# A four-layer graph network on one core: TensorE's large operations planned in two parts, with a new order table

## The chip, the cores and the metric

The kernel runs on one core of a Trainium2 chip. The metric is the device time of one execution in microseconds (us), as the median of several runs. The engines are named as in the profile: PE is TensorE's matrix multiplication, PEld its weight loads, DVE VectorE, ACT ScalarE, POOL GpSimd and SP SyncE, which here only issues DMAs.

## What is computed

There are 16 graphs of 1024 nodes with 256 features each (float32), and one adjacency matrix of 1024 x 1024 for all. Four layers follow each other. Each normalises x, applies a ReLU and adds the result of a graph layer:

```python
h = jnp.maximum(_layernorm(x, axis=-1), 0.0)
x = x + _L0_gnn_ref(h, adj, L0_gnn_W, L0_gnn_a)    # and so on: L1, L2, L3
```

Layers 0 and 1 are graph attention with one head. The score of a pair is the sum of a term of each node, and the weights are masked by adj and normalised over the neighbours:

```python
h = jnp.matmul(inp, W)
e = jax.nn.leaky_relu(e_src[:, :, None] + e_dst[:, None, :], negative_slope=ALPHA)
e = jnp.where(adj[None, :, :] == 0, NEG_INF, e)
h_prime = jnp.matmul(jax.nn.softmax(e, axis=-1), h)
```

Layer 0 ends in a ReLU, layer 1 in an ELU. Layer 3 is the same with four heads of 64 features and an ELU. Layer 2 is a transformer block: queries, keys and values from one 256 x 768 matrix, eight heads of 32 features, scores q k / sqrt(32) masked by adj, softmax, sum with the values, a layer norm, a feed-forward part (256 to 256, ReLU, 256 to 256) and another layer norm.

## The kernel before

**Stages.** A stage is one layer of one graph, so there are 64. `order` (L1844 on) interleaves them: in the middle of the run, layer 2 of graph b, layer 1 of graph b+1, layer 3 of graph b and layer 0 of graph b+2 follow each other, and the preparation of a later stage overlaps the main part of an earlier one.

**Way in** (`way_in`, L1100). Each tile of 128 nodes gets its moments (DVE L1047, L1048, or ACT L1071), the inverse root on POOL (L1051 and L1052, or L1074 and L1075) and the normalisation (ACT L1135 or L1151, DVE L1144). Four tiles, half a graph, make one call of `transpose_rows` (L1083): eight PE transposes (L1090) into one pair of PSUM banks, which ACT empties into `hT` (L1093). Then come the projections, all through `project` (L1095, its matmul is L1097): `gat_values` (L1194) two tiles at a time for layers 0, 1 and 3; `two_values` and `queries_keys` for layer 2. ACT or DVE empties each product's bank pair.

**Main part.** Layers 0 and 1 (`gat_item`): DVE makes the weights p of a tile of neighbours (L1362), PE multiplies them with the values (av, L1379), and ACT and DVE finish each tile (L1396 to L1422) and hand it to the next layer's way in. Layer 3 (`pair_item`): weights on DVE (L1443), values and sums as 32-column matmuls that run four at a time (L1477, L1501). Layer 2 (`dot_item`): PE makes the scores of four heads as four concurrent 32-row matmuls into two pairs of banks (sc, L1597), ACT exponentiates them (L1611), DVE masks them (L1619), and PE multiplies with the values (acc, L1628). Every second time POOL issues a DMA that adds one block of weights to the next (L1645), and a matmul forms the sums of what has landed (L1658). After the last neighbour `dot_out` normalises, and `feed_forward` (L1739) and `finish` do the rest: transposes, the up product with ACT's ReLU (L1774), the down product with DVE's addition (L1797), the second layer norm (L1812, L1819).

**Buffers.** PSUM's eight banks are two single accumulators ("acc") and three pairs ("u"). Transposes, projections and scores all take pairs from these three, and one score operation takes two.

**What sets the order.** Nothing is issued in the order in which the code above is written. Each piece of work is an `op` with an engine, a cost in us, a rank, the operations that it comes after, and the buffers that it takes and ends. After all are collected, `play` (L941) runs `forward` (L839), a planner that lays the operations out in time engine by engine with these costs, with `DELAY` (L769) from the end of an operation to its users on other engines, and with `SWITCH` (L772) added on PE when the form of the matmuls changes (full, 32 rows, 32 columns):

```python
DELAY = (0.2, 0.12, 0.14, 0.06, 2.0, 1.4)   # PE, DVE, ACT, POOL, SP, QUEUE
SWITCH = {None: 0.2, 132: 0.21, 32: 0.125}
```

Of the operations that could begin within `SLACK` (0.5 us) of the earliest, the one with the lowest rank goes first. The instructions are then issued in the planned order. The ranks come from the text `RANKS` (L47), three characters for each operation; it is used if its length is three times the number of operations, and otherwise `play` makes ranks by planning forward and backward eight times. QUEUE is not an engine but the planner's picture of POOL's DMA queue: the adding DMA is planned as 0.9 us on POOL with a delay of 0.6, then 5.2 us of QUEUE and its delay.

Of the kernel before, what the change touches and what calls it, by code (L numbers as in the profile page):

```python
# [28 lines left out]
U8 = mybir.dt.uint8  # L29
# [3 lines left out]
AX = mybir.AxisListType  # L33
PSUM = bass.MemoryType.PSUM

P = 128
# [11 lines left out]
    "$7K#`;$57#};#U[#8d#-f##%###$'v#;a#.U##$#$5#$&$6j#Pq#$(#cE##E#$W#$<#xV##=#%#$Jw#$;##,#$H#$o#+$#Jm#$w#+d##+#%?$1;"  # L48
    "#H)#&R#')#'C#'O#'.#':#'R#'b##f#+###3##r$=O##I##j#*}##H##v#*b#Tz#cL#`U##0##6##C#$I#$G#$T#Gf#$7##5#$F#iA#$_##-#%)"
    "##y#ok##F##|##G##h#$'#`@#*-#$-#*i#`R#S$#WI#$}#%U##4#%x#$[#$Z##z#$E#$i#$2#%p#we#$O#%t#*j#*`#$A##&#$C#)>$&R$<_#vY"  # L50
    "$<6#JZ#%V#)u#)2#$K#(K#(-#wg#%h#&4#&%#&]##x#$Q##u##.#%l#%z#$@##P#$|#''#$a#-m#$]#]<#'?#%:#$D$BL#$j#]:#%7#&Y$H;#&8"
    "#%D$19#$:#AB#%u#&?#}=#&S#%9#%_#',#&A#'-#&q#v_#$P##Y#&B#%i#&w#'g#&`#'7#%n#'I#_p#L=#b##$h#$p##L#$u#$q#$y#%%#$L##W"
    "#%-#%W#%<#%`#'a#'6#&(#%3#%d#&t#cA#%J#&H#A:##R#%[#%k##9#'U#%s##`#,L#'&##S#%g#$4#'`#%B#%v$#8##c#%f#&z#c:#$e$Iu#Xf"
    "$*R#&9#%}#Xg#&:#_/$-O#uE#%G#*g#EY#T8#ui#$c$CA$H8#$n#3%#Tp#%F#2b#%@#${$Ew#&C##b#%M#$f#$0#%H#$z#$%#%/#$l#%4#$M#%N"
    "#%8#%e##(#&I#%+#t<#j?#%,$.f#&M#%.#2?#]0##n#'E#$v#%$#$t#$m#%m#%^#'j#(m#'H#(d#$x#&*#&[#&o#%q##J#']#-@#%P#%1#'Q#vX"
    "#EX#:B#$.#%I##7#$d#%a##_##8#$3#'W#'{#&'#/r#%=#az$KE#$b#'4#L`#$$#b$#0:#_0$*r#R9#$##&m#+q#*$#09#&u$*q$Kt#&1#'>#05"
    "$7h#R8#%0##a#0F#[F#'T#&i#$J#G>#&e#_g#ov#(,#GS#(}$:)#&K#%r#&^#%A#&n#&&#%&#$B$8R#&v$Ks#&j$LG#Fy#'%#JJ#&/#)P#&$$(M"
    "#&p$08#uH#tF#o7#)O#&F#%o#%b#&+#*(##X$9B#&>#%O$9##'|$9Y#DY#$>#'P#'_#'l#(5#)@#'}#?+#%6#(6#Y.#[N#[M#<R#0j#(##%2#q_"
    "#qN$9n#*M##K#&c#&b#'=#$R#1Q##Z##2#o4#$*#($#$?#(/#%R$9p#oM#&V#I8#-2#DZ#Kr#1d#,B#&G#'9#Jq#*q#$8$9v$:_#y7#6?#'f#K="
    "#(s#r:#(r#'*$Bb#_s$%L#([#JM#(<#AL#(I#w_#r5#&E#&P#(%#,_#(*#VI$+d#'c#'q#KL#.-#(f#-V$4l$Je#'r#((#;3#H+#<&#)#$?&#AO"  # L60
    "#ck#(8#&O#vO#83$5F$:^$7.#(.#(C#&g#(J#&=#(R#)K#(V#(l#(U#)0#)%#)|#)D#)S#+2#;7#%w#&a#$)#'1#&_#%*#$`#(7#(X#%y#(y#i*"
    "#&h#u,#re#(_#(W$0=$23$0<#&U$FK#&T#(L#(2#K##(D$/n#)r#0n#(A#(v#(N$0;#)q#(0#)p#0m$8Y#)3#)-#Gq#4f#)x#)E$$A#=Q#G]#'L"
    "#i+#H8#'d$3a#Jy#()#)/#)8#'t#)b#(a$8u#vv##B#)1#)9#D,#)g#,q##A#vo##@#)6#)Y#)7$Ho#)+#QW#uq#),#(@#)d#'F#$N#)*$=##)C"
    "#+k#*:#*s#,g#-r#+0#71#0t#0(#(|#q<#D4#pz#D:#*>#)R$6w#(e#QZ#D(#,.#)G#`-#*T#*9#*a#.j#,1#*B#*H#*l#Dk#LC#*'#-j#*W#'["
    "#u4#*Q#*4#{s#-h#D3#9J#*_#*J#p|#B##La#.8#*v$5.#7I#+4#*[#eE#.D$IK#*u#*U#*S#)h#.>#(P#.<#*X$;}#+B#=B#+R#*h#nE$+q#(O"
    "##]#*f#*]$5?$Ij$M.#+m#+>$5%#u3#+Q#+<$L]#>x#Ig#+l#*V#+=#/'#[p$B@#<;#+^$-|#Y_#+Y#*%$B?#zG#XR#K{#+L#+&#+c$O%#+j#<_"
    "#+i$4}$<>#+u#*y#)_#y($Ai#}A#+g#+]$C,$6m#Wb#L%#,,#M=#aC#{a#+5#rn#,>#C/#+`#+[$Ek#?>#*8#,f$0H##D#)4#)T#*K#+|#jE#+%"
    "#&X#,n$G;#,'#(G#..#e2#+b$7r#?k#Qu#)L#g9#*m#on#nl#.Z#+-#=R#Jt#.'#.]#-x#.H$E4#H@#-U#-a#/_#.G#.P#0.#-]#l;#*x#/V#/L"
    "$(9#.O$OJ$Dr#.I#/f##<#0B#.N#^T#/9#.*#-W#.r#.9#1)#0<#/U#.S$A:#D1#fV#;2#/3#.;#+,#+*$<H#y)#Va$9G#+f#,/$Ah#*<#LD$7-"
    "#,*#VV#T&#,9#-+$?)$Bc#M<#C'#{>#)W#rY#Cn$:i#Cm#,C$-{#T%#,o#,7#/,$7D#4e#+C#,^#,6#/.#+a$:h#)}#,v#aB#['#,V#+M#&W#,N"  # L70
    "#0g#?R#-Q#,d#.,#,;#+)#?Q#-O#0-#(F$Oa#+O#+.#(h#,}#*P#,u$Dz#-$#.0#,Z#l4#-&#,D#+9$7;#-?#,j#(g#-%#]s#,0$/$#+w#m:#,h"
    "#]e#,8#-=$?3#RV#0D#-N#nI$Mt$7v##*$G=#-y#,a#.V#Ht#/4#,M#(`#p9$(y#.J#l<#+1#,W#:a#/b#,e#om#*7#-q#*R#+H$Do#*w#1+#+G"
    "#/z#,l#-u#,z#,|#.R#.$#-(#*/$>o#.a#oP#.:#--#/%#+K#-B#/>#._#-X#.^#o,#.b#.v#Qz#BC#mJ#QP#0h#`=#-G$J{$Kv#(M#&s$5D#.A"
    "#&r#0$#)m#1P#,y$J0#1Z#0+#&-#-w#be#,{#/}#*O#/k#-A#&)#,U#/g#,(#+z#/5#0)#h0#,`#-p#,r#'2#,X#.C#g0#/t#0k#u$#0/#/{#-^"
    "#+_#.{#/6#/K#/Y#/X#1&#*e#.B$,_#]3#_(#oN#(b#0l#VS#)`#)^#*Z#*&#,?$0z#+/#+h#,k#*t#*,#*G#**#*L#(3#8+$8;#*)#+($59$J|"
    "#WB$.g$J_#yG#+e#)n#+:#-;#)o#+3#-e#,O#LX$0E#2J#+D#*A#I3#*z#dg#.=#s,#s-#.w$/X#+E#,J#*C#+7#/+$'I#Tk#A-#)l#+o$6d$#`"
    "#,x#|=#)B#-S#-_#-I#-|#-}#-v#)?#/l#+}##?#0U#S:#^S#0X#2M$(x#-8#.t#.h#9|#-R#mG#ff#.d$CJ#(H#/H#:.#t##/0#/($B;$)K#/#"
    "#[?$=C#[a#-K#/[#.K#.u$7m#,Q$5H#,G#mt#/v#,F#3D$5G#jF$KK$>T#.p#2D#od##>#S;#2E$CI#.q#q^#Kz#.7#0>#//#.E#EF#Sr#0*#hd"
    "#tv#f?#P0#-*#0E#0C#/8#,&#/^#mu$=<#-t#0?#2Y#l&#/J$<;#mA#{f#/o#Ci#-M#8`#1J#3,#29#`D#0L#if#ie#pF#0G#;p#{H#8k#/)#]?"
    "#_<#[z#+;#+Z#+T#+{#30#1*#1i#,R#+N#+U#Do#1;#./#ol#q}#/y#H&#31#qH#-o#)Z#.4#Gk#}x#4K#/T#Yz#0`#0K#15#.[#2o#1j#0H#.&"  # L80
    "$J3#/x#0]#,##+J#/P#/Q$'V#0r#0Z#0z#1?#1$#1F#1R#0[#1/#0f#/$#11#1>#03#5.#1E#1:#2m#1[$N-#1o#0o#@-#(Y#5<#);#b4#1(#aA"
    "#1z#6]#7Y#/1#-c#1Y#^6$JQ#1e#/7#12#1C#Se#2*$;s#@1#H^$*{#0x#-b#0p#9y#1k#?b#/]#1y#(Z#1f$BO$-i#e-#tJ#2&#/&#cO#0S#5;"
    "#1g$1/#2=$Hh#1h#bj#0b$-h$*T$*(#2B$*6$+|#0|$JU#2)#1=$*4#{*#2T$K7#2X#2(#1^#@.#M%#2O#/e#/m#5'#p{#2^#0%#/d#4E#7e$K6"
    "#53#2G$+T$>W#21#1n#/Z#S)#-k#A+#0^#1B#-1#T.#nV#6W#2[#>%$@p#2Z#2'$Iw#58#1`#[-#1s#2C#,t#]b$Iv#,:#4O#46#M'#26#/?#nW"
    "#(k#pq#2$#2:#2Q#oX#^v$$m#.1#3/#Hk#>$$>V#0M#>B#1m#3;#.F#2A#3C#3>#2_#3M#4D#3T#/G#3Q#42#3U$-]#3N#8n#3v#9f#3P#8j#5q"
    "#?I#44#)i#6t##[#2@#`<#4]#(?$1m#5`#4J#*N#4T#33#OG#*Y#7.#:*#,K#50#L1$C4#t'#U+#*E#R*#7)#1D#zf#zI$-u#1I#/A#8.#5X$Cp"
    "#3B#wq#/E#kJ#37#3i#2|$26#4;#7U#35#7^#:>#59$;,#5x#4x#7=#7L#3L#1q#B9#[w#qy$5Z#2h#2N#oL#WY#OF#[v#43$Bg#4s#3##1x#B'"
    "#o6#D7#,5#2d#2f#mK$'$#K,$#o#3.#3t$?6#1|#07#Ju$OZ#?P#3K#^<#2e#bA#32#mM$'G$EU#3[#4r#2z#25#b_#3A$-?#3R#HV#23#1T#3G"
    "$=J#2W#2##+@#3s#L9#4>#3+$M,#3W#2n#3e#2y#3?$*f#3Z$+R#3]#e5#47#$,#5a#3'#-i#34#+?#1l#3^#17#9S#3f#3<#3u#3w$Mg##l#TB"
    "#2x$1Q#3x#4j#41#4&#2w#J6#4-$7G#4I#40#3g#3@#4Z#3m#70#F|$4s#GO#4<#4,$;Q#B>#7/#6O#4|#BQ#4m#<C#uo$Ld#5_$C8#4?#1<#4N"  # L90
    "#24#3d#4P$.*#5C#6s#3=#4l#5Q$8E#5>#80#3O#-F#69#4k#3}#-E#5O#Be$I|#'D$5/#^V#3S#s`#2l#5h#94#1G#76$?T#5W$Ec#7N#1p#5L"
    "#5y#Bm#By#9W#9k#$1#Br#1,#6a#Bl#5V$Eg#6v##o#7?#6w#f@#Av##e#uz#/i#3|#0J#0O$O$#0T#1t#5s#0P#7##2F#V3#0R#Mm$IW#2{#61"
    "#[4#2]#[0$?H$?A$?R#Bs#F{#6(#6P#6'#zP#Mz#6&#4Q#4=#4C#4y$03#7@#(x#4U#oZ#3($A-#5]#1S#l##4B#tj$+P#T2#5%#51$;Y#60#4F"
    "#X%#s@#5)#5B#36#4:$60#Y=#5o#49#5b#1W$1h#nw#5{#9##78#X9#aw#4%#6j#5z#6n#R,$FF#Qw#5H#5S#7R#2R#fi#6|$6$#r0#5R#5j#Bf"
    "$7+#4##7m#77$IX#5n#6-#6z#7(#7A#W=#6b#}t#6Y#75#hw#W2#hv#yy#7$##^#6Q$Bi#Nj#Vr#o5$*x#Dd$3z#5/#5,#4{#5i#0Y#F7#62#5$"
    "#3*#.T#7z#8O#6d#3c#-s#.W#6i#6u#5##5^#.s#.6#6Z#XQ#6m#6x#r)#7B#O:#7u#2S#79#8U#7i#:?#{N#9O#9h#%K#7g#7V#@9#nv#7|#%]"
    "#8G#7[#6^#8;#85#7k#8-#8S#8D#8B#7v#68#9,#M;$9,#TE#8b#?a#8a#;##8H#9&$>)#<q#8J#_q#Lm$'3#HE#,$#7C#2p$4.#7'#k8#nm#7D"
    "##'#Y0#7G#5v#Em#8R$JF#8&#5g#3V#6o#6{#7%#8N#6D#7a#7t#7P#7K#4^#6G#7T#6;$)%#Y@$El#4w#7-#k`#7d#7x#:8$JE#4*#4v#7J$Kh"
    "#9$#l=#5U#8X$1j#7;#7+#7{#4t#3I#4i#:;#SW#G(#45#4h#@]#@[#Ks#:x#9H#;x#9'#x-#x]#;w#:v$<7#7_#Z&#87#d1$@?#g+#d6#6`#8'"
    "#:P#nX#'e#mW$F<#<6#8s#9Z#<p$>-#-4#86$Eh#<)#6N#98#cl#-g#cq#Ln#Ft#;r#9B#0I#9l#8F#9=#9:#:r#:)#9i#9%#2.#2-$N}#5k#74"  # L100
    "#'m#'z#_M#8E#:o#9?#9M$ER#K7$/m#5[#@W$0,#9D#9[#cp#8e$Ej#/R#F.$,u#9g#9A#&k#:l$,t#<##@_#G&#/D$({#'<#;}#xH#9Y#?p#';"
    "#9R#:I#9d#2r#:s#6K#Ab#8K#&2#:H#8u#;o#I>#x'#9Q#:t#93$#a$#n#8P$/p#;V#mX$+G$B0#95#7p#;U$=h$HX#9E#Fe#;s#:e#9z#9<$IZ"
    "#Cj$3S#84#:4#:9#xo#:(#yc#9{#@^#[A#:y#9K#&3#IB#8w#x.#:`##;#8v#I@#7M#um#:k#cB#Z,#;5#9}$16$,Z#QY#=$#;M#6e#Qb#ns$K-"
    "$,Y#:d#8$$Ki#dk#;=#9>#:=#J:#89#?'#9t#6)#:<#jC#9;#em#;@$DX#<A#;C#9u#:c#4[#;N#el#;1#6I#<8#4n$DP#:}#;k#AX#uT#;P#5J"
# [515 lines left out]
def fast_path(tc, bad, x, adj, l0_w, l0_a, l1_w, l1_a, w_qkv, ln1_g, ln1_b, ln2_g, ln2_b, w1, b1, w2, b2, l3_w, l3_a, out):  # L620
# [13 lines left out]
    with ctx:  # L634
# [128 lines left out]

        ops = []
        PE, DVE, ACT, POOL, SP, QUEUE = range(6)

        DELAY = (0.2, 0.12, 0.14, 0.06, 2.0, 1.4)  # L769
        ITSELF = 0.04  # L770

        SWITCH = {None: 0.2, 132: 0.21, 32: 0.125}  # L772


        BEFORE_END = 0.1
# [1268 lines left out]
```

## Time and profile before

| | us |
|---|---|
| three runs | 4212.40, 4209.66, 4214.54 |
| median | 4212.4 |
| the profiled execution, whole | 4213.85 |
| its span, first to last instruction | 4212.1 |
| PE busy | 4093.9 |
| DVE, ACT, POOL busy | 3170.0, 2322.9, 1169.6 |
| PE's waits for the adding DMA (L1658) | 27.8, in 35 waits |
| mean granted clock of PE | 0.994 |

In a line of the groups, the part between "x" and "|" is the number of instructions, then come busy time and the mean of one in ns, then the engine's idle time just before them with what ended it. In a line of the timeline, the first number is the start in us, the second the time from the first start to the last end of the instructions merged in the line, and the bracket holds the idle time before. A float32 matmul is recorded as two instructions. Matmuls overlap in the record, so that the time from one start to the next says more than the length of one. In a line of the stretches, the last three numbers are the granted clock as a share of the full one, the DMA engines' busy share and GB/s; before them stand the length and the busy times of PE, PEld, DVE, ACT and POOL with their counts.

### The profile page before, as it was taken

The numbers are of one execution on the slowest core, as the hardware profiler recorded it, in microseconds if no ns is written. First come the engines' busy times: TensorE is split into PE (matmuls) and PEld (weight loads), VectorE is DVE, ScalarE is ACT, GpSimd is POOL, SyncE is SP. The second block draws the span as 40 slices with busy tenths as digits, with TensorE's granted clock in tenths as the row PEclk, the third lists the DMA queues.
The fourth block names the chain that finished last, engine by engine and source line by source line (L and its number), as shares of the span: only waits on it lengthen the run. The fifth ranks groups of instructions, "written<-read, shape, count | busy, mean of one in ns | idle before, by whom it ended". The sixth has DMA issues, their size and how long they took to land.

```text
span 4212.1 us, 67534 instructions
## 1 busy us (share of the span) xinstructions
PE 4093.9 (97%) x25993; PEld 2160.5 (51%) x25993; DVE 3170.0 (75%) x5964; ACT 2322.9 (55%) x4235; POOL 1169.6 (28%) x2025
## 2 busy tenths in 40 slices
PE   8999999999999999999999999999999999999997
PEld 7735255553555536455364654546545465564433
DVE  7577867778677786777867778776787877859697
ACT  5564645636456364564646646465463745666452
POOL 2322231412314123141331423223132241423131
PEclk9999999999999999999999999999999999999999
DMA  3171814518145181451815518164271733636361
GB/s 124 34 158 35 176 45 96 111 49 170 39 99 107 51 170 36 112 108 37 170 38 116 113 35 162 41 135 91 53 151 33 159 67 79 121 82 132 72 135 47
DMA packets 106826, 398.96 MB, mean 95 GB/s; under 512 B 11528, under 2 KB 47744, under 8 KB 73728
## 3 DMA queue, kind: packets, MB, share of 16 engines
q0 software_dynamic: 46080, 302.01, 36.5%
q1 hardware_dynamic: 60000, 92.03, 6.7%
q8 instruction: 206, 3.38, 0.3%
q14 instruction: 124, 1.02, 0.1%
q10 hardware_dynamic: 416, 0.52, 0.0%
HBM read 107.87 MB, written 18.21 MB: 30 GB/s over the span
## 4 chain that ended last, share of the span: by engine, by line
PE 74%; DMA 7%; DVE 6%; issue 6%; ACT 4%; POOL 2%; SPq 0%; POOLq 0%; ACTq 0%; DVEq 0%
PE pm L1097 19%; PE av L1379 18%; PE acc L1477 10%; PE sc L1597 8%; PE acc L1628 6%; DMA pe<-pe 5%; PE sums L1501 5%; PE sums L1658 3%; PE tp L1090 3%; DVE pe L1619 2%; DMA y<-offsets 2%; ACT pe L1611 1%; DVE y L1797 1%; ACT pm L1071 1%; PE tpv L1540 1%
## 5 line engine op out<-in xcount | busy, mean ns | idle before, releaser
L1619 DVE TENSOR_TENSOR pe<-pe,mask 128x1024 f32<-128x1024 f32 x1024 | 1200.6, 1219 | 208.7 <-ACT pe L1611 205.1
L1611 ACT ACTIVATE pe<-sc 128x1024 f32<-128x1024 f32 x1024 | 998.0, 1022 | 321.0 <-PE sc L1597 228.0
L1379 PE MATMUL av<-v,p 128*128 128x257 f32 x4096 | 956.7, 384 | 21.7 <-ACT o L1402 10.7
L1379 PEld LDWEIGHTS av<-v,p 128*128 128x128 f32 x4096 | 764.9, 191 | 210.9 <-issue 60.8
L1443 DVE SCALAR_TENSOR_TENSOR p<-r,e,mask 128x1024 f32<-128x1024 f32 x512 | 623.0, 1274 | 114.6 <-DMA r<-kept 98.0
L1597 PE MATMUL sc<-qT,kT 32*128 32x512 f32 x4096 | 620.9, 642 | 2.7 <-ACT pe L1611 1.5
L1628 PE MATMUL acc<-pe,v 128*32 128x512 f32 x4096 | 538.3, 604 | 1.3 <-DVE pe L1619 0.6
L1645 POOL DMA_DIRECT2D pe<-pe x256 | 224.7, 878 | 992.5 <-PE acc L1628 628.7
L1074 POOL TENSOR_SCALAR rstd<-stats 128x1 f32<-128x1 f32 x512 | 159.0, 311 | 1153.4 <-ACT xn L1071 739.8
L1477 PE MATMUL acc<-p,v 128*32 128x512 f32 x4096 | 463.0, 593 | 0.0
L1597 PEld LDWEIGHTS sc<-qT,kT 32*128 32x128 f32 x4096 | 189.8, 183 | 379.4 <-issue 174.7
L1097 PE MATMUL pm<-l_wx,hT 128*128 128x259 f32 (+1 forms) x1536 | 369.5, 389 | 8.1 <-ACT hT L1093 5.2
L1362 DVE SCALAR_TENSOR_TENSOR p<-r,e,mask 128x512 f32<-128x512 f32 x512 | 349.1, 743 | 24.8 <-DMA r<-kept 19.1
L1075 POOL TENSOR_TENSOR rstd<-rstd,minus_half 128x1 f32<-128x1 f32 x512 | 331.6, 648 | 42.7
L1097 PEld LDWEIGHTS pm<-l_wx,hT 128*128 128x128 f32 x1536 | 287.4, 191 | 79.1 <-ACT hT L1093 20.7
L1658 PE MATMUL sums<-pe,pick 128*32 128x512 f32 x2048 | 269.5, 603 | 28.6 <-DMA pe<-pe 27.8
L1477 PEld LDWEIGHTS acc<-p,v 128*32 128x32 f32 x4096 | 131.1, 110 | 296.1 <-issue 282.1
L1628 PEld LDWEIGHTS acc<-pe,v 128*32 128x32 f32 x4096 | 94.2, 108 | 339.8 <-issue 206.4
L1051 POOL TENSOR_SCALAR rstd<-stats 128x1 f32<-128x1 f32 x256 | 131.9, 515 | 454.5 <-DVE stats L1048 450.8
L1501 PE MATMUL sums<-p,e 128*32 128x512 f32 x2048 | 242.3, 593 | 0.0
L1097 PE MATMUL pm<-hT,qkv_sb 128*128 128x512 f32 x512 | 228.6, 593 | 2.6 <-ACT hT L1093 2.3
L1052 POOL TENSOR_TENSOR rstd<-rstd,minus_half 128x1 f32<-128x1 f32 x256 | 207.8, 812 | 21.3
(122 smaller groups left out, 4133.0 us busy)
## 6 DMA issues: line engine op xcount, KB each, us to landing
pe<-pe POOLq DMA_DIRECT2D x256, 1024.0 KB, 8.7
r<-kept SPq DMA_DIRECT2D x64, 512.0 KB
x<-in_x_dram SPq DMA_DIRECT2D x32, 512.0 KB
x<-offsets POOLq DMA_DIRECT2D x32, 512.0 KB, 5.5
y<-offsets POOLq DMA_DIRECT2D x32, 512.0 KB, 5.8
out_dram<-x SPq DMA_DIRECT2D x64, 256.0 KB
r<-kept SPq DMA_DIRECT2D x62, 256.0 KB
edges<-in_adj_dram SPq DMA_DIRECT2D x8, 512.0 KB
```

What stands on the lines that cost most here:

```text
L1075: nc.gpsimd.tensor_tensor(rh.t, rh.t, minus_half, ALU.pow)
L1097: nc.tensor.matmul(dst, lhsT=lhsT[:, k, :], rhs=rhs[:, k, :], start=(k == 0), stop=(k == KC - 1))
L1362: nc.vector.scalar_tensor_tensor(ph.t[:, j % each, :], rh.t, s.e[:, j, H + h : H + h + 1], mask[:, j, cols], ALU.max, ALU.mult)
L1379: nc.tensor.matmul(avh.t[:, : s.hs + 1], lhsT=phs[part].t[:, j % each, i * P : (i + 1) * P], rhs=s.v[:, j, h, :], start=(j == 0), stop=(j ...
L1443: nc.vector.scalar_tensor_tensor(ph.t[:, hh, :], s.rh[hp].t[:, hh, :], s.e[:, j, col : col + 1], mask[:, j, :], ALU.max, ALU.mult)
L1477: nc.tensor.matmul(acc[n].t[(2 * hh + part) * W : (2 * hh + part + 1) * W, :], lhsT=s.v[:, jj, h, part * W : (part + 1) * W], rhs=p, start ...
L1501: both(lambda jj, n, hh, h, p: nc.tensor.matmul(sums.t[(2 * n + hh) * W : (2 * n + hh + 1) * W, 0, :], lhsT=s.e[:, jj, 2 * H + h : 2 * H + ...
L1597: nc.tensor.matmul(scs[pair].t[:, hh, :], lhsT=s.kh.t[r0 : r0 + D2, g, j * P : (j + 1) * P], rhs=s.qh.t[r0 : r0 + D2, g, cols], start=True ...
L1611: lambda pair=pair: nc.scalar.activation(part(pair), scs[pair].t, AF.Exp, scale=SCALE2),
L1619: lambda pair=pair: nc.vector.tensor_tensor(part(pair), part(pair), masks(), ALU.mult), [ex], tiles=True,
L1628: nc.tensor.matmul(head(acc, i), lhsT=s.v[:, j, g * QUAD + i, :D2], rhs=ph.t[:, i, :], start=(j == 0), stop=(j == NT - 1))
L1658: nc.tensor.matmul(head(sums, i), lhsT=pick[:, g, :], rhs=th.t[:, i, :], start=first, stop=last)
```

## The change

The transposes of half a graph and all projections of two banks become two operations of the planner each, of half the cost; the second comes after the first. The matmuls, their operands and their banks stay. Whoever read a product after the whole of it now comes after the part that writes what it reads, in `gat_values`, `feed_forward` and `finish`; where one instruction empties both banks (`transpose_rows`, `two_values`, `queries_keys`) it comes after the second part. Some twenty costs and one delay are set anew, and `RANKS` is replaced by a longer text (343 lines for 329).

```diff
-        DELAY = (0.2, 0.12, 0.14, 0.06, 2.0, 1.4)
+        DELAY = (0.2, 0.12, 0.14, 0.06, 2.0, 1.8)
...
-            m_op = op(DVE, 0.54, rank, stats, after, takes=[mh, rh, *takes])
-            r_op = op(POOL, 1.1, rank + 0.6, root, [m_op], ends=[mh])
+            m_op = op(DVE, 0.55, rank, stats, after, takes=[mh, rh, *takes])
+            r_op = op(POOL, 1.4, rank + 0.6, root, [m_op], ends=[mh])
...
-            q_op = op(ACT, 0.49, rank + 0.4, square, after, takes=[rh, *takes], ends=ends)
-            r_op = op(POOL, 1.4 if shift else 1.15, rank + 1.0, root, [q_op], ends=[mh])
+            q_op = op(ACT, 0.52, rank + 0.4, square, after, takes=[rh, *takes], ends=ends)
+            r_op = op(POOL, 1.5 if shift else 1.2, rank + 1.0, root, [q_op], ends=[mh])
...
-            def turn():
-                for u, src in enumerate(srcs):
-                    for k in range(KC):
-                        nc.tensor.transpose(tph.t[:, k, u * P : (u + 1) * P], src()[:, k * P : (k + 1) * P], ident)
-
-            a = op(PE, 0.88, rank, turn, after, takes=[tph], ends=ends)
-            return op(ACT, 0.92, rank + 1.1, lambda: nc.scalar.activation(dst.t, tph.t, func, scale=scale), [a], ends=[tph])
+            a = []
+            for half in range(2):
+
+                def turn(half=half):
+                    for u in range(2 * half, 2 * half + 2):
+                        for k in range(KC):
+                            nc.tensor.transpose(tph.t[:, k, u * P : (u + 1) * P], srcs[u]()[:, k * P : (k + 1) * P], ident)
+
+                a.append(op(
+                    PE, 0.44, rank + 0.5 * half, turn, (after[2 * half : 2 * half + 2] if len(after) == len(srcs) else after) + a,
+                    takes=[] if half else [tph], ends=ends,
+                ))
+            return op(ACT, 0.92, rank + 1.1, lambda: nc.scalar.activation(dst.t, tph.t, func, scale=scale), a, ends=[tph])
...
-                    ACT, 0.4, rank,
+                    ACT, 0.49, rank,
                     lambda: nc.scalar.activation(src(), xt(), AF.Relu, scale=rh.t, bias=mh.t[:, 1:2]),
...
-            for u, t in enumerate(ts):
+                vals = op(
+                    PE, 0.88, rank + 0.9 * u, product, [turned] + ([s.vals[0]] if t else []) + [vals] * u + weights_in[s.layer],
+                    takes=[] if u else [pmh] + ([] if t else [s.vh, s.eh]), ends=[hT],
+                )
                 s.vals[t] = vals
                 gat_scaled(s, t, (lambda u=u: pmh.t[:, u]), pmh, width, rank + 2.0 + u, vals)
...
-                add = op(DVE, 0.46, rank + 0.9, add_one, [o], takes=[mh], ends=[oh], tiles=True)
+                add = op(DVE, 0.54, rank + 0.9, add_one, [o], takes=[mh], ends=[oh], tiles=True)
...
-                add = op(DVE, 0.95, rank + 1.3, add_both, [o], takes=[mh], ends=[eh, oh], tiles=True)
+                add = op(DVE, 1.08, rank + 1.3, add_both, [o], takes=[mh], ends=[eh, oh], tiles=True)
...
-            a = op(PE, 3.43, rank, up, [turned], takes=[pmh], ends=[xh])
-            ups = [
-                op(
-                    ACT, 0.58, rank + 3.6 + 0.6 * m,
+                a = op(PE, 1.715, rank + 1.8 * m, up, [turned] + [a] * m, takes=[] if m else [pmh], ends=[xh])
+                ups.append(op(
+                    ACT, 0.58, rank + 2.0 + 1.8 * m,
                     lambda m=m: nc.scalar.activation(uh.t[:, m, :], pmh.t[:, m, :], AF.Relu, bias=b1_sb[:, m, :]),
...
-            a = op(PE, 3.48, rank, product, ups, takes=[pmh], ends=[uh])
+                a = op(PE, 1.74, rank + 1.8 * u, product, ups + [a] * u, takes=[] if u else [pmh], ends=[uh])
...
-                c = op(DVE, 0.8, rank + 3.7 + 4.0 * u, add, [a, shifted[0]], takes=mhs)
+                c = op(DVE, 1.05, rank + 3.7 + 4.0 * u, add, [a, shifted[0]], takes=mhs)
...
-                        DVE, 0.5, at + 3.0, add_scaled, [centred, r_op, shifted[1]], takes=[nh], ends=[s.yh, rh], tiles=True
+                        DVE, 0.64, at + 3.0, add_scaled, [centred, r_op, shifted[1]], takes=[nh], ends=[s.yh, rh], tiles=True
```

`two_values` and `queries_keys` are cut in the same way, into two operations of 1.74 and of 1.715 us.

## The prediction

> **What bounds the kernel now.** I read the page first, then TensorE's own waits, then short stretches of the timeline.
>
> ```profile
> PE 4093.9 (97%) x25993; PEld 2160.5 (51%) x25993; DVE 3170.0 (75%) x5964; ACT 2322.9 (55%) x4235; POOL 1169.6 (28%) x2025
> ...
> PE 74%; DMA 7%; DVE 6%; issue 6%; ACT 4%; POOL 2%; SPq 0%; POOLq 0%; ACTq 0%; DVEq 0%
> ```
>
> TensorE (PE) is busy 97% of the span and three quarters of the chain that ended last are its own. Only what makes PE do less, or wait less, can move the end. The 118 us in which it shows no instruction (4212.1 - 4093.9) are not all of the slack, because matmul records overlap. So I worked out PE's pure work from the timeline, by the steady distance from one start to the next: 4096 x 217 ns (the attention products av), 1024 x 218, 512 x 226, 512 x 216, 512 x 216, 512 x 429 and 256 x 429 (the projections, L1097), 2048 x 109 (transposes), which is 2002 us. The 32-row and 32-column matmuls run four at a time, 429 ns a round: 4096 rounds are 1757 us, and each of the 512 score operations (sc, L1597) is about 0.1 us longer than its two rounds, 51 us. All together, with the masks' start: 3813 us. Changing between full, 32-row and 32-column matmuls happens 1352 times in the timeline and costs 91 to 116 ns each: 146 us. Before the first matmul pass 7.6 us, after the last real one 16 us. Of the span that leaves 4212 - 3813 - 146 - 24 = 229 us of stalls. That is all that an order of the work can win without fewer form changes. TensorE's waits name part of it:
>
> ```profile
> PE sums L1658 <- DMA pe<-pe: 27.8, 35, 2.5
> PE pm L1097 <- ACT hT L1093: 15.0, 18, 1.4
> PE tp L1090 <- ACT xn L1151: 13.3, 9, 7.6
> PE av L1379 <- ACT o L1402: 10.7, 9, 5.6
> PE tps L1677 <- ACT sums_sb L1668: 7.4, 5, 5.7
> ```
>
> The columns are total us, times, longest. All such waits come to 106 us; 7.6 (the start, in the third line) and 7.2 (the closing check) are outside the scheduled body, so 28 us wait for the gather DMA and 63 for results of ACT, POOL and DVE. The rest of the 229 is inside operations. Two stretches show how:
>
> ```profile
> 2028.36 1.31 PE L1597 MATMUL sc<-qT,kT 32*128 32x512 f32 x8
> 2029.61 1.07 PE L1628 MATMUL acc<-pe,v 128*32 128x512 f32 x8
> 2033.02 1.62 PE L1658 MATMUL sums<-pe,pick 128*32 128x512 f32 x8 [2.35 <-DMA pe<-pe]
> 2034.57 2.09 PE L1597 MATMUL sc<-qT,kT 32*128 32x512 f32 x8
> ...
> 1112.89 3.62 PE L1097 MATMUL pm<-qkv_sb,hT 128*128 128x256 f32 x16
> 1116.35 1.04 PE L1090 MATMUL tp<-ident,y 128*128 128x128 f32 x8
> 1118.54 1.13 PE L1097 MATMUL pm<-qkv_sb,hT 128*128 128x256 f32 x4 [1.16 <-ACT hT L1093]
> ```
>
> First: the gather lands late, PE idles 2.35 us, and then runs slowly (1.62 us for eight sums, elsewhere 1.07). Second: a whole transpose, then 1.16 us of nothing, since ACT was still emptying the value product of 1112.89 before it could empty the transpose. The stretch from 2033.4 shows the slow clock:
>
> ```profile
> 2033.40:2036.80 3.40, 3.40 (x20) 0.72 (x16) 2.36 (x2) 1.73 (x3) 0.00 (x0) 0.50 1.02 212
> ```
>
> The 0.50 is the granted clock. Nine such stretches lie in the body, 41 us, some 36 of them busy: 18 us lost.
>
> **What the Trainium skill says.** "TensorE: Matmul & The Clock Gate", Part 1: after an idle window of about 3.4 us the array falls to half clock. The trace agrees in the half, but a gap of 2.35 us was enough here. "TensorEngine Tiling (Array Packing)", Key Properties: changing the tiling mode drains the engine; the trace shows the 91 to 116 ns. "Perfetto Trace Analysis", Identifying the Most-Contended Engine: matmul busy time is a bad measure of nearness to the limit; agreed, 97% busy is 3813 / 4212 = 91% work.
>
> **The change part by part.**
> *Instructions.* None is added: each large operation is issued as two parts with the same matmuls. The table tells the count: 36,462 characters are 3 x 12,154, 37,998 are 3 x 12,666, and 512 more operations are exactly the cuts (transposes 160, L0/L1/L3 products 192, queries and keys 64, values, up and down 32 each). So the new table is used. Work stays 3813 us.
>
> *Durations.* They only steer the planner, but the old ones are short of the rows:
>
> ```profile
> L1151 ACT ACTIVATE xn<-x,stats 128x256 f32<-128x256 f32 x256 | 124.0, 505 | 159.7 <-DVE stats L1048 156.1 <-ACT mask L1894 0.6
> ...
> L1051 POOL TENSOR_SCALAR rstd<-stats 128x1 f32<-128x1 f32 x256 | 131.9, 515 | 454.5 <-DVE stats L1048 450.8 <-DVE inv L1396 2.7
> L1052 POOL TENSOR_TENSOR rstd<-rstd,minus_half 128x1 f32<-128x1 f32 x256 | 207.8, 812 | 21.3
> ```
>
> Norm 0.505 (planned 0.40, now 0.49), POOL's root 0.515 + 0.812 = 1.33 (1.1, now 1.4). On DVE the corrected durations add 128 x 0.14 (the scaled residual, L1819) + 128 x 0.08 (layer 0's, L1407) + 128 x 0.13 (layer 1's, L1421 and L1422) + 64 x 0.25 (the down product's, L1797) = 61 us that the old order did not provide for. PE's own durations were right already: sc then acc is planned as 1.08 + 0.98 = 2.06 and the timeline has 1.085 + 0.996.
>
> *Gather waits.* Planned 0.9 + 0.6 + 5.2 + 1.4 = 8.1 us, now 8.5; issue to landing is 8.7 at the median, 7.6 and 10.0 at the quartiles. So 0.4 us covers few of the late ones. I take a third of 28: -9 (bounds 0 and -20).
>
> *Waits for ACT, POOL and DVE.* A half transpose needs two of the four norms; the first bank of a GAT, up or down product can be read half a product (0.88 or 1.74 us) sooner; and a half fits where 3.48 us did not. In the second stretch, half the value product behind the transpose would hide the 1.16 us. I take two fifths of 63: -25 (0 and -45). What is late next there is ACT's emptying of the bank, which values, queries and keys still do in one piece after the second half.
>
> *Waits inside sc and acc.* Sc before a 32-column operation averages 1.203 against 1.071 at its fast tenth (389 times, 51 us); with acc's own and sc before full work, 77 us. They wait for ACT's exponentials and DVE's masks, which a 3.48 us product keeps starved. I take a quarter: -19 (+15, if halves hold one of the three bank pairs longer, and -40).
>
> *Half clock.* Fewer gaps of 2 us: 7 of 18 (0 and -14).
>
> *Form changes.* A half put between sc and acc costs 0.109 + 0.094 - 0.113 = 0.09 us more than none, between two acc 0.21. One cut in four so parted: 128 x 0.09 = +12 (0, and 512 x 0.09 = +46).
>
> *Added waits.* The second half follows the first on PE, in order, with no wait for another engine but its two norms. SP's and POOL's DMAs move with the order only; the mask and offset transfers keep their causes.
>
> Sum: -9 - 25 - 19 - 7 + 12 = -48. Against the profiled execution, 4213.85 (span 4212.1 and 1.75 around it), 4166; this execution was 1.45 over the median of 4212.4, so I put 4164 for the median.
>
> **The rivals.**
> *Much more is won* (0.14): correct durations and small parts take most of 186 us (28 + 63 + 77 + 18): 70% is -130, with +10 of changes about 4090. For it speaks that PE's planned durations fit so well; against it that the gathers' spread and sc's dependence on three bank pairs stay. Case range 4060 to 4125.
> *Nothing moves* (0.14): the order trades stalls for form changes, -45 and +40: 4207. DVE at 75% and ACT at 55% speak against a new bound.
> *Slower by parting* (0.17): the cuts are spread through the score stretches. At 400 parted halves, half of them at 0.09 and half at 0.21, +60 us, against no more than 35 won: 4237. It decides from about 300 parted halves. For it: the old order already enters full work from 32-wide forms 283 times. Against it: the planner charges 0.2 us for each entry, more than the trace's 0.09.
> *The change does not do what it says* (0.01): excluded by the count above.
>
> **How the numbers follow.** The likeliest case has 0.54, 4125 to 4200. Faster by over 0.2% (about 8 us, what a measurement of this kernel can tell from no change) is that and the large win, 0.68, and a little of the slight cases, 0.02; within 0.2%: 0.13; slower: 0.17. The range 4095 to 4230 holds the likeliest case, half of the large win, the unmoved one and a third of the slower: 0.54 + 0.07 + 0.14 + 0.06 = 0.81. The likeliest case's own range stands beside it because cases of both signs are in.
>
> **What would show it.** Right: PE's instructions still 25993 and starts as far apart as before; waits for ACT, POOL and DVE down from 63 to near 40; sc's mean before 32-column work nearer 1.15; fewer than nine half-clock stretches; form changes near 1480. Wrong: form changes over 1650, sc's mean over 1.25 with banks held longer, or the gathers' 28 us grown because sums follow their issue sooner.

## The result, and the profile after

| | kernel before | changed kernel |
|---|---|---|
| median of four runs each, us | 4213.47 (4209.66 to 4217.30) | 4240.74 (4238.04 to 4242.57) |
| ratio | 1 | 1.0064, 95% interval 1.0049 to 1.0079 |
| the profiled execution, whole / span, us | 4213.85 / 4212.1 | 4241.77 / 4240.0 |

The changed kernel is 27 us slower. The forecast was 4164, and the range ended at 4230. The page's first part and its chain of engines:

```profile
PE 4113.6 (97%) x25993; PEld 2138.2 (50%) x25993; DVE 3171.5 (75%) x5964; ACT 2333.0 (55%) x4235; POOL 1206.7 (28%) x2025
...
PE 74%; issue 7%; DVE 6%; DMA 6%; ACT 5%; POOL 2%; SPq 0%; POOLq 0%; ACTq 0%; DVEq 0%
```

No engine does more instructions than before, and neither line names a cause. TensorE's waits say more (columns: total us, times, longest):

```profile
PE sums L1685 <- DMA pe<-pe: 16.8, 23, 1.9
PE tp L1107 <- ACT xn L1171: 14.2, 9, 8.6
PE tp L1107 <- ACT y L1783: 11.2, 8, 3.7
PE av L1406 <- ACT o L1429: 10.3, 11, 1.9
PE tps L1704 <- ACT sums_sb L1695: 7.5, 9, 2.9
...
PE pm L1117 <- ACT hT L1113: 6.9, 12, 1.3
...
PE pm L1117 <- ACT v L1264: 2.8, 5, 0.9
PE pm L1117 <- ACT e L1246: 2.7, 5, 0.7
...
PE pm L1117 <- DVE v L1270: 2.4, 4, 0.8
```

The gather's waits fell from 27.8 to 16.8 us, and those for the emptied transpose (`hT`) from 15.0 to 6.9, as forecast. But the last three lines are of a kind of which the kernel before shows a single wait (1.1 us, for an `e`). A product `pm` waits for the instructions that read `pm`: the exponential `e` and the scaled values `v`, both made from a product that is already done.

The planned durations were corrected, and the measured ones of these rows stayed where they were, except that one kind of POOL's roots grew (0.531 + 0.931 us; before 0.515 + 0.812; the other kind, L1088 and L1089, stayed at 0.97):

```profile
L1066 POOL TENSOR_TENSOR rstd<-rstd,minus_half 128x1 f32<-128x1 f32 x256 | 238.2, 931 | 21.3
L1065 POOL TENSOR_SCALAR rstd<-stats 128x1 f32<-128x1 f32 x256 | 136.0, 531 | 424.2 <-DVE stats L1062 422.6
L1171 ACT ACTIVATE xn<-x,stats 128x256 f32<-128x256 f32 x256 | 124.0, 504 | 187.4 <-DVE stats L1062 181.5 <-issue 3.0
```

A stretch of the timeline that stands for the prediction's two, and below it the granted clock of the end of it (0.51):

```profile
1027.52 0.44 PE L1107 MATMUL tp<-ident,y 128*128 128x128 f32 x2
1029.34 0.44 PE L1107 MATMUL tp<-ident,y 128*128 128x128 f32 x2 [1.38 <-ACT y L1783]
1029.71 2.08 PE L1624 MATMUL sc<-qT,kT 32*128 32x512 f32 x8
```

```profile
1030.80:1034.20 3.40, 3.40 (x9) 1.18 (x4) 3.40 (x4) 2.13 (x3) 0.47 (x1) 0.51 0.97 192
```

The second part of a transpose waits 1.38 us for one of its two norms. That wait the prediction had allowed for.

The sum, worked out anew in the prediction's way (work from the steady distance between starts; a form change by its kind; the rest is stalls; its rows come out within 3 us of the prediction's), for both kernels and for the first experiment below:

| us of the profiled execution | before | changed | changed, banks apart |
|---|---|---|---|
| pure work and the two ends | 3839 | 3840 | 3839 |
| form changes (number) | 143 (1352) | 151 (1430) | 151 (1430) |
| stalls | 230 | 250 | 175 |
| of these, PE's waits for the gather | 27.8 | 16.8 | 19.4 |
| of these, PE's waits for ACT, POOL and DVE, without the start and the closing check | 63.6 | 81.8 | 38.0 |
| half-clock stretches in the body (total length) | 9 (41) | 7 (27) | 3 (17) |
| mean of sc before 32-column work (times) | 1.203 (389) | 1.176 (363) | 1.171 (363) |

So +8 of form changes and +20 of stalls make the 28 us between the spans.

### The profile page after: what moved, and what is told of

Read it like the earlier page. It is cut to its first block, busy times and chain, and to the rows that moved or that the text cites. A ratio compares the mean times of both kernels' runs of the same rounds, so it can differ in the third digit from the quotient of the medians.

```text
span 4240.0 us, 67624 instructions
## 1 busy us (share of the span) xinstructions
PE 4113.6 (97%) x25993; PEld 2138.2 (50%) x25993; DVE 3171.5 (75%) x5964; ACT 2333.0 (55%) x4235; POOL 1206.7 (28%) x2025
## 4 chain that ended last, share of the span: by engine, by line
PE 74%; issue 7%; DVE 6%; DMA 6%; ACT 5%; POOL 2%; SPq 0%; POOLq 0%; ACTq 0%; DVEq 0%
PE pm L1117 19%; PE av L1406 18%; PE acc L1504 10%; PE sc L1624 7%; PE acc L1655 6%; PE sums L1528 5%; DMA pe<-pe 4%; PE tp L1107 3%; DVE pe L1646 3%; PE sums L1685 2%; ACT pm L1085 1%; ACT pe L1638 1%; DVE y L1825 1%; PE tpo L1704 1%; PE tpv L1567 1%
## 5 line engine op out<-in xcount | busy, mean ns | idle before, releaser
L1088 POOL TENSOR_SCALAR rstd<-stats 128x1 f32<-128x1 f32 x512 | 158.9, 310 | 1209.3 <-ACT xn L1085 712.5
L1117 PE MATMUL pm<-l_wx,hT 128*128 128x259 f32 (+1 forms) x1536 | 380.7, 390 | 13.9 <-ACT v L1264 2.8
L1089 POOL TENSOR_TENSOR rstd<-rstd,minus_half 128x1 f32<-128x1 f32 x512 | 335.2, 655 | 42.7
L1685 PE MATMUL sums<-pe,pick 128*32 128x512 f32 x2048 | 270.2, 602 | 17.4 <-DMA pe<-pe 16.8
L1066 POOL TENSOR_TENSOR rstd<-rstd,minus_half 128x1 f32<-128x1 f32 x256 | 238.2, 931 | 21.3
```

What stands on the lines that cost most here:

```text
L1089: nc.gpsimd.tensor_tensor(rh.t, rh.t, minus_half, ALU.pow)
L1117: nc.tensor.matmul(dst, lhsT=lhsT[:, k, :], rhs=rhs[:, k, :], start=(k == 0), stop=(k == KC - 1))
L1685: nc.tensor.matmul(head(sums, i), lhsT=pick[:, g, :], rhs=th.t[:, i, :], start=first, stop=last)
```

## What the cause could be

The new waits can be followed in the program itself. "Perfetto Trace Analysis", Identifying Dependency Chains, in the Trainium skill, says to look at an instruction's text for the semaphores on which it waits. Done for every second part of a product: of the 352 products that are cut, 140 second parts wait for an instruction that reads the bank of the first part (131 on ACT, 9 on DVE). In the kernel before there is none. Both banks are one buffer, `pmh`, and the program's dependencies are drawn for the buffer as a whole. While a product was one operation, all its readers came after it and this did not show. Now a reader may stand between the two parts. Where it stands ahead of the second part, PE waits for it; where it stands behind, the reader waits for the second part, though its own bank was ready at least 0.9 or 1.7 us before. In the changed program 164 instructions that touch only the first bank wait for a matmul of the second; in 71 of these cases PE does other work between the two parts. This second kind is not new: in the kernel before, 171 such instructions wait for the second bank's matmuls. The statement that a reader now comes after the part that writes what it reads thus holds in the planner's list, and not in the program. The planner knows neither wait.

**Theory 1:** these waits are what the change loses by, and without them the forecast holds. **Theory 2:** the new order is fitted so closely to the planned durations that POOL's longer roots (planned 1.2 to 1.4 us) and other misjudged ones show in full. **Theory 0:** each cut costs by itself. **Theory 3:** the 78 more form changes. The "replay" in the expectations is the planner's own arithmetic over a fixed order, with the waits put in or left out.

One pair of up products shows the readers' side. In the changed kernel the eight matmuls of both parts run without a break from 1856.95 (the first part ends at 1858.83), but ACT's ReLU of the first bank starts at 1860.58, after all of them, as it does in all 32 pairs of the kernel before:

```profile
1856.95 3.60 PE L1117 MATMUL pm<-hT,w_sb 128*128 128x512 f32 x8
...
1860.58 0.69 ACT L1802 ACTIVATE hT<-pm,b_sb 128x512 f32<-128x512 f32 x1 [2.29 <-PE pm L1117]
...
1861.66 0.67 ACT L1802 ACTIVATE hT<-pm,b_sb 128x512 f32<-128x512 f32 x1
...
1862.12 3.62 PE L1117 MATMUL pm<-w_sb,hT 128*128 128x256 f32 x16
...
1865.78 0.42 DVE L1825 SCALAR_TENSOR_TENSOR y<-y,pm 128x256 f32<-128x256 f32 x1 [6.67 <-PE pm L1117]
```

DVE then waits in the same way for both parts of the down product (6.67 us idle, ended by `pm`). Another down product shows PE's side: its second part stands still for 0.61 us until DVE has read the first bank twice (2653.14 and 2653.68, done at 2654.09):

```profile
2651.43 1.67 PE L1117 MATMUL pm<-w_sb,hT 128*128 128x256 f32 x7
...
2652.94 0.60 PE L1107 MATMUL tp<-ident,y 128*128 128x128 f32 x4
2653.14 0.42 DVE L1825 SCALAR_TENSOR_TENSOR y<-y,pm 128x256 f32<-128x256 f32 x1 [7.35 <-PE pm L1117]
...
2653.68 0.41 DVE L1825 SCALAR_TENSOR_TENSOR y<-y,pm 128x256 f32<-128x256 f32 x1
...
2654.15 1.99 PE L1117 MATMUL pm<-w_sb,hT 128*128 128x256 f32 x8 [0.61 <-DVE y L1825]
```

## The experiments

**The banks apart.** The instructions, their order on every engine, table and costs are those of the changed kernel. Between two instructions on different engines that touch different banks of one `pmh`, the dependency is taken out (in `gat_values`, `feed_forward` and `finish`; nothing is shared between them, so no order is lost). "PSUM — Partial Sum Buffer", PSUM bank collisions raise a hardware error, asks to guard PSUM by bank and quadrant or, simpler, by bank. The pair is more than that, and the 0.61 us above were spent on a bank that PE did not write.

```diff
+        def by_bank(h, u, *made):
+            seen = h.__dict__.setdefault("seen", [])
+            for i in made:
+                for v, was in seen:
+                    if v != u and was.engine != i.ins.engine:
+                        tc.declare_no_dep(i.ins, was, reason="other bank")
+            seen.extend((u, i.ins) for i in made)
...
-                    project(pmh.t[:, m, :], w1_sb[:, :, m * P : (m + 1) * P], xh.t)
+                    by_bank(pmh, m, *project(pmh.t[:, m, :], w1_sb[:, :, m * P : (m + 1) * P], xh.t))
```

> The changed kernel, same instructions in the same order on every engine. Only the waits between different banks of one PSUM pair are gone, in the values of the GAT layers, the up products and the way back: a second half no longer waits for readers of the first half's bank, and a reader of the first bank no longer waits for the second half's product. Theory 1 (the halves wait for each other through the pair they share, which the planner doesn't know): replaying the order with the planner's costs gives 42 us less without these waits, so 4190 to 4215 us, with the idle time before second halves that stand apart down from 28 us to under 12. Theory 2 (the order has no slack, and the longer roots on GpSimd and other misjudged durations show in full): 4232 to 4242, no change beyond 8 us. Theory 3 (the 78 more form changes): no change.

Measured: 4169.0 us, ratio to the kernel before 0.9894 (0.9879 to 0.9909). That is 72 us under the changed kernel and 44 under the kernel before; it lies below the expected range, which rests on the replay's 42.

The gaps that the profile shows on PE before second parts of products that stand apart from their first fell from 9.9 us (17 gaps) to none. The 28 us of the expectation are counted otherwise. A count from one start to the next, with the form changes in it, gives 28.9 us for the changed kernel and 13.9 here. The gain does not come from issuing fewer instructions: the program has 2919 separate semaphore instructions, the changed kernel 2918. The 1430 form changes are still in, 8 us more than before, so theory 3 explains at most those. The same two places (by their count among the pairs) now read:

```profile
1828.10 3.60 PE L1117 MATMUL pm<-hT,w_sb 128*128 128x512 f32 x8
...
1830.01 0.69 ACT L1812 ACTIVATE hT<-pm,b_sb 128x512 f32<-128x512 f32 x1 [0.57 <-PE pm L1117]
...
1831.73 0.69 ACT L1812 ACTIVATE hT<-pm,b_sb 128x512 f32<-128x512 f32 x1 [0.54 <-PE pm L1117]
...
1833.27 3.62 PE L1117 MATMUL pm<-w_sb,hT 128*128 128x256 f32 x16
```

```profile
2605.63 1.89 PE L1117 MATMUL pm<-w_sb,hT 128*128 128x256 f32 x8
...
2607.56 0.42 DVE L1835 SCALAR_TENSOR_TENSOR y<-y,pm 128x256 f32<-128x256 f32 x1 [7.35 <-PE pm L1117]
2607.80 1.89 PE L1117 MATMUL pm<-w_sb,hT 128*128 128x256 f32 x8
```

The first ReLU starts 1.91 us after the product's start instead of 3.63, and the second part of the down product no longer waits for DVE, which began 0.24 us before it. The page's first part, the chain and the longest waits of this kernel:

```profile
PE 4081.6 (98%) x25993; PEld 2138.7 (51%) x25993; DVE 3173.0 (76%) x5964; ACT 2341.1 (56%) x4235; POOL 1201.3 (29%) x2025
...
PE 79%; DMA 6%; issue 6%; DVE 5%; ACT 2%; POOL 2%; SPq 0%; POOLq 0%; ACTq 0%; DVEq 0%
```

```profile
PE sums L1695 <- DMA pe<-pe: 19.4, 31, 2.5
PE tp L1107 <- ACT y L1793: 10.4, 7, 3.7
PE tp L1107 <- ACT xn L1181: 9.1, 2, 8.5
...
PE pm L1117 <- ACT hT L1113: 3.0, 7, 1.1
```

PE's share of the chain rose from 74% to 79%, and ACT's fell from 5% to 2%.

**The cut alone.** The changed code with the order of the kernel before written out, the two parts of each product back to back. (The table holds every operation's place; the planner's choice is replaced.)

```diff
-            for _ in ops:
-                at, o = choose(open_ops, time, begin, rank, SLACK)
+            for o in sorted(ops, key=lambda o: rank[o.number]):
+                at = max(begin(o), time[o.eng])
```

> The changed kernel's cuts and code, but the order of the kernel before on every engine, the two halves of a product back to back. This is the cut alone, without the new order. Theory 1: a cut costs nothing by itself, since with the halves back to back the readers come after both anyway: 4203 to 4220 us against 4213 of the kernel before. A rival (theory 0): each cut costs TensorE the 0.16 us that the planner charges for a dependent operation on the same engine, some 43 us in the replay, so about 4255.

Measured: 4212.8 us, 1.0002 (0.9994 to 1.0011), with 1352 form changes. A cut by itself costs nothing that shows (at most 5 us by the interval); theory 0 is out.

**The wait moved to the readers.** The same written-out loop with the changed kernel's order on every engine; only which of two engines' instructions is written down first differs.

> The changed kernel with each engine's order untouched; only the order in which the program is written down differs, so that a second half stands ahead of the readers of the first half's bank (135 of 147 such readers). The wait then passes from TensorE to the readers: they wait until the second half is done. Theory 1: readers that come late release their followers late, the replay with these waits gives 137 us more than for the changed kernel, so well slower than 4241, 4300 to 4400. Theory 2, under which these waits don't matter: 4235 to 4245.

Measured: 4352.9 us, 1.0334 (1.0315 to 1.0353). The same instructions in the same order on each engine are 2.6% slower than the changed kernel when the readers do nearly all the waiting (eight second parts still wait for a reader). The row of the ReLU, for this kernel, the changed one, the one with the banks apart and the kernel before (the number after the second bar is ACT's idle time before it, nearly all for `pm`):

```profile
L1802 ACT ACTIVATE hT<-pm,b_sb 128x512 f32<-128x512 f32 x64 | 42.1, 684 | 109.4 <-PE pm L1117 109.4
```

```profile
L1802 ACT ACTIVATE hT<-pm,b_sb 128x512 f32<-128x512 f32 x64 | 42.9, 685 | 88.4 <-PE pm L1117 88.3
```

```profile
L1812 ACT ACTIVATE hT<-pm,b_sb 128x512 f32<-128x512 f32 x64 | 44.0, 688 | 69.3 <-PE pm L1117 68.9
```

```profile
L1774 ACT ACTIVATE hT<-pm,b_sb 128x512 f32<-128x512 f32 x64 | 40.7, 683 | 60.7 <-PE pm L1097 60.7
```

The first three have one order and can be compared; the last has another, in which other instructions stand before the ReLU. From the end of the first part to its ReLU it takes 2.76 us on average here, 1.01 in the changed kernel, 0.04 with the banks apart and 2.00 in the kernel before (32 pairs each).

**The roots made light.**

```diff
-                nc.gpsimd.tensor_tensor(rh.t, rh.t, minus_half, ALU.pow)
+                nc.gpsimd.tensor_tensor(rh.t, minus_half, minus_half, ALU.mult)
...
-        nc.vector.tensor_copy(bad, count[:1, :1])
+        nc.vector.memset(bad, 0)
```

> The changed kernel with the inverse roots left out: GpSimd multiplies two constants where it raised to a power (the normalisation is thereby a constant), and the flag at the end is set to pass. All waits, orders and other work stay. Theory 2: the roots on GpSimd, planned at 1.2 to 1.4 us and 0.85 to 2.2 in the trace, cost about 34 us in a replay of the changed order, so 4200 to 4212. Theory 1 alone: the roots have slack to be late in, 4230 to 4240.

Measured: 4229.9 us, 1.0041 (1.0026 to 1.0056), with POOL busy for 906 us instead of 1207. That is about 11 us under the changed kernel, at theory 1's edge, and the two intervals just overlap. The roots are not the main cause: with the power gone from all of them, 17 of the 27 us stay. Other misjudged durations, which theory 2 names too, were not tried one by one; they are all still in the kernel with the banks apart, which is 44 us faster than the kernel before.

**One side at a time.** The condition of `by_bank` gets `and i.ins.engine == mybir.EngineType.PE` in the first, `!=` in the second.

> The changed kernel, where only TensorE is freed: its second halves no longer wait for readers of the other bank (140 such waits), but a reader of the first bank still waits for the second half's product when it stands after it. Theory 1a (what costs is TensorE's own wait, the 28 us of idle time seen before second halves): 4195 to 4215 us. Theory 1b (what costs is the readers that come late, and what hangs on them; in the replay this side is 38 of the 42 us): 4230 to 4242.

Measured: 4220.7 us, 1.0016 (1.0009 to 1.0022).

> The mirror of the run before: readers of the first bank no longer wait for the second half's product, but TensorE's second halves still wait for the readers that stand ahead of them. Theory 1a: 4215 to 4235 us. Theory 1b (replay: 2.5 us above the kernel with both sides free): 4168 to 4180.

Measured: 4180.7 us, 0.9919 (0.9906 to 0.9932). Freeing PE gives 20 us, freeing the readers 60, both 72. The two are not a sum: PE's side is worth 20 us taken first and 12 taken last, the readers' 60 or 52. The readers' side is the larger, as theory 1b has it, but PE's is not nothing: the first time lies between the two ranges, the second 0.7 us above that of 1b. The waits that the profile shows most plainly, on PE, are the smaller part of the price.

The first of the two also says where the 27 us come from. With PE freed, the readers are still tied as they were in the kernel before, and by the table's sum some 228 us of stalls are left, as before (230); the kernel is then about as much slower than the kernel before (7 us) as the added form changes cost (8 us). So most of the slowdown is PE's new waits, and the readers' ties are the gain that did not come.

**Only the feed-forward part by bank** (the 32 up and 32 down pairs; `gat_values` as in the changed kernel).

> The changed kernel with both sides freed, but only in the feed-forward stage of the transformer layer: 32 pairs of up products and 32 of the way back. The 192 pairs of the GAT layers' values keep their waits (111 of TensorE's 140). Replay: the GAT pairs' waits alone cost 15 us of the 42, so 27 gained, and with the measured 72 for all about 46: 4190 to 4200 us. If the gain went by the number of pairs (64 of 256), 18: about 4223.

Measured: 4197.1 us, 0.9958 (0.9945 to 0.9971). A quarter of the pairs gives three fifths of the gain. These pairs have a long run of work after each reader (ReLU, down product, addition, second norm, next layer), which may be why; that was not tried.

**The order of before, by bank.** The second experiment's kernel with the first one's edit.

> The cuts in the order of the kernel before, halves back to back, with both sides freed as in the first run. If the gain of the first run over the kernel before comes from readers that start a half earlier whatever the order: 4170 to 4190 us. If it needs the new order (the replay gives 8 us for freeing alone here): 4202 to 4210.

Measured: 4183.9 us, 0.9932 (0.9920 to 0.9944). The replay's 8 us were wrong, 29 are gained; why the replay is so far off here while it sorted the pairs well stays open. With it there are four times (medians) that can be read together:

| | order of the kernel before | new order |
|---|---|---|
| cut, banks tied | 4212.8 | 4240.7 |
| cut, banks apart | 4183.9 | 4169.0 |

With the banks tied the new order loses 28 us, with the banks apart it wins 15. So of the 72 us, 29 can be had in the old order too, and 43 are what the ties cost the new order beyond that.

## Why the prediction was wrong

**The step that failed** is "Added waits": "The second half follows the first on PE, in order, with no wait for another engine but its two norms." 140 second parts got a wait for ACT or DVE that no product of the kernel before has; freeing them alone gives 20 us. A second step fails with it, under the -25: "the first bank of a GAT, up or down product can be read half a product (0.88 or 1.74 us) sooner". 164 instructions on the first bank are still tied to the second (171 before); freeing the readers gives 52 to 60 us. I took the dependencies from the planner's list (`after`, `takes`, `ends`), which has the readers behind the right part, and did not ask what the buffer itself draws: one `pmh` for two banks. With these waits taken out and nothing else, the time is 4169.0 against 4164 forecast. This cause is shown, by the experiment with the banks apart and the two that free one side.

**Waits for ACT, POOL and DVE** (-25): in the changed kernel they grew by 18 us, from 63.6 to 81.8. With the banks apart they fell by 26, to 38.0; in the order of the kernel before they fall to 42.0 by freeing alone, so this term hardly needs the new order. The idea, that a bank can be read half a product sooner, was right; it was just what the shared buffer forbade. In 18 of the 32 up pairs the first ReLU started only after the second part; before in all, with the banks apart in none.

**Gather waits** (-9): -11 in the changed kernel, -8 with the banks apart. **Half clock** (-7): nine stretches became seven, 41 us became 27, so 7 us less lost at half clock; with the banks apart three stretches and 17 us, so 12 less. **Waits inside sc and acc** (-19): sc's mean before 32-column work fell to 1.176, not to 1.15, and with fewer such changes its excess over 1.071 from 51 to 38 us; the direction held.

**Form changes** (+12 for one cut in four parted): 380 of the 512 second parts don't follow their first directly in the new order, far over the rival's point of 300, but the changes grew only by 78, +8 us. Between the two parts of 310 of them lie only full-width matmuls, where parting changes no form. The rival *slower by parting* named 4237, 4 us from what was measured, and its mechanism was wrong all the same (60 us of form changes, where 8 came): a rival that ends on the right number is not thereby shown.

**Instructions, work, durations**: right. PE still has 25993 instructions and the work is the same within 1 us. One kind of POOL's roots is longer than planned (1.46 against 1.4), the other shorter (0.97 against 1.2); together they cost about 11 us at most. None of the three signs that the prediction named for being wrong came (1430 form changes, sc's mean 1.176, the gather's waits 16.8 us); the one sign for being right that failed is PE's waits for ACT, POOL and DVE.

**The sum** was -48; with the banks apart the span is 46.9 us shorter (+8 of form changes, -55 of stalls). The forecast described that kernel, not the one it was made for. That it comes within 5 us there is in part luck: of the 44 us under the kernel before, 29 need no new order at all, and the terms were estimated as fractions, a third, two fifths, a quarter.

## What to carry to other kernels

When an operation is cut so that its readers can start sooner, look at the buffer and not only at the listed dependencies: if both parts are in one tracked buffer, each reader is tied to the other part, on one engine or on the other, depending on which is written down first. Count such waits in the program's semaphores before trusting a plan that doesn't know them. Count them in the kernel before, too: a tie that was there already is a gain that the cut will not bring. And don't judge them by the idle time of the busiest engine alone: freeing the readers alone gave three times what freeing PE alone did (60 us against 20).

## What the runs showed of the hardware

**The half clock.** The length of a single gap on PE does not decide it. In the changed kernel a gap of 1.38 us (1027.96 to 1029.34) came before a stretch at half clock (0.51 from 1030.8 on), and one of 2.87 us (to 790.29) before none: the clock was 1.00 from 785.1 to 795.3. So that 2.35 us "was enough" in the kernel before is one case and no threshold. The stretches begin on a grid of 3.41 us: from 771.4 to 1030.8 and from there to 1290.3 are 76 steps each. PE was busy for 59% of the step before the stretch of 1030.8, and for 47% of the step from 788.5, which none followed; what decides stays open.

**POOL beside DVE.** POOL's power instruction (L1066), with unchanged code and shapes, took 0.931 us on average in the changed kernel and 0.812 before. This goes with the order: in the six profiles that have the new order and the power in it, it is 0.907 to 0.931, in the three with the old order 0.808 to 0.812. In the trace it goes with what DVE does meanwhile. Of the 256 in the changed kernel, the 17 beside no DVE instruction took 0.57 us; the 122 that lie mostly beside one of DVE's two mask products took 1.22 (`p`, 68 of them) and 1.39 (`pe<-pe,mask`, 54). Before, 100 lay beside one. No run here moved the one and left the other.
